# Layer-1 FFN of a vision tower: tokens normed and turned in the attention, results turned by VectorE and DRAM, pieces in a new order, and six attention buffers

## The chip, the cores and the metric

The kernel runs on one core of one Trainium2 chip. A core has TensorE (PE; PEld is its weight load), VectorE (DVE), ScalarE (ACT), GpSimd (POOL) and SyncE (SP), each with its own queue that is worked off in order; here SP issues nearly all transfers. The metric is the device time of one execution in microseconds (us); the time before is the median of three runs.

## The reference

32 images of 3x256x256 are cut into 256 patches of 16x16, and each becomes a token of 256 features. Two layers follow, each an attention and an FFN with a layer norm ahead of it and a residual around it. Layer 0 is a gated attention and a gelu FFN on 127 chosen tokens. Layer 1's attention works with phases (sine and cosine) and a causal sum. Layer 1's FFN is the last stage:

```python
sx = einsum('bsh,ndh->bnsd', x, hl_w) + hl_b          # 4 heads of 64
q = einsum('bnsd,neod->bneso', sx, wq)                # 4 experts
scores = einsum('bnesd,bntd->bnest', q, k) * d ** 0.5 + causal
out = softmax(scores) @ v                             # then gated over experts: mixed
resid = sx[arange(nh), arange(nh)]                    # image n, head n, for every image
hn = layernorm(mixed + resid, ln_g, ln_b)
hx = relu(fx @ fc1_w.T + fc1_b) @ fc2_w.T + fc2_b     # fx: hn by heads
fout = layernorm(hx + fx, fnorm_g, fnorm_b)
return fout * softmax(fout @ fgate_w.T) by heads
```

x is the normed token; the result is added to the unnormed one.

## The kernel before, in words

All 32 images stay in SBUF (`H`, tokens on the partitions, features along the row). The stages follow each other: patches to tokens (A), layer-0 attention (B), layer-0 FFN (C), layer-1 attention (D, to about 1245 us), layer-1 FFN (E, to the end). In all of them the order of instructions on each engine is the order in which the program is written. A matmul needs features on the partitions, so tokens must be turned first.

**Two ways of turning.** `feature_major` turns one image with four 128x128 transposes on TensorE into a bank of PSUM, and another engine copies them out. `blocks_turned` turns 32x32 blocks on VectorE and writes them to DRAM; `moved` reads them back with the blocks in their places, and gives a view of the tile in which runs of 32 columns lie 128 apart. B, C and D use the second way.

**Stage D** works on pairs of images, in steps t; `do(s, f)` runs f for pair u where t = 3u + s. So each f comes up once in three steps, and a pair passes: `norm_d`, `blocks_d` and `moved_d` (s = -1), `residual_d` on GpSimd (1), `hidden` (2, gelu), `phases` (3, tanh and sine: dturn, dz), `match` (4, dat), `memory` (5, reads the normed tokens dx), `output` (6), `add_output` and `stats_e` (7). dx has four buffers, two pairs. `norm_d` of a pair stands after `memory` of the pair two before it, whose buffers it takes. The first two pairs are normed in stage C; pair 0's tile dxT is loaded at step 1.

**Stage E** is cut into 93 pieces (`PIECES`), most of them on one engine. `ROUND` is one round, written out by hand: entries (-back, piece), so that image r + back has its piece in round r. Nine images are in flight. From `heads` of the last image on, the order is that of the list `END`. The pieces that matter here:

- `tokens` (VectorE, ex, L175) norms an image's tokens, `turn` (TensorE, L808) turns them, `turned` (ScalarE, exT, L1108) copies them out, and `heads` multiplies by hl. For the first four images `heads` also makes the residual `res`.
- `mixed` 0 and 1 (VectorE and GpSimd, L1289), `summed`, `squares`, `root`, `scaled` give er. `turn_e` turns er on TensorE, and `turned_e` (ScalarE, fxT, L1331) copies it out with the norm's factors.
- `features_moved` and `first_layer_out` move halves into the tile both by DMA; `second_layer` multiplies by W2; `head_gate` (small VectorE products, L1382 to L1406) and `last_norm` (VectorE L1411, L1414, L1425; GpSimd L1417, L1422) end the image. `later_keys` (GpSimd, L1208) masks the scores.

Weights of E are made in `prepare`, between the matmuls of stage C. After the images a check of value ranges decides whether a general path must be run (not in these executions).

Of the kernel before, what the change touches and what calls it, by code (L numbers as in the profile page):

```python
# [33 lines left out]
F32 = mybir.dt.float32  # L34
# [19 lines left out]
for _name, _k in [  # L54
    ("b_u", 4), ("b_base", 1), ("gamma", 2), ("beta", 2), ("b1", 8), ("bk1", 2), ("bq1", 2),
    ("bk2", 1), ("bq2", 1), ("ln_w", 2), ("ln_b", 2), ("hl_b", 2), ("fc1_b", 1), ("freq", 1),
    ("e_g", 1), ("e_b", 1), ("fn_g", 1), ("fn_b", 1), ("fc2_b", 1), ("attn_g", 1),
]:
    COLS[_name] = (_n, _k)
    _n += _k  # L60
# [20 lines left out]
def vit_tower(tc, a, out):  # L81
# [12 lines left out]
    H = [cpool.tile([P, NC, D], F32, name=f"h{b}") for b in range(B)]  # L94

# [517 lines left out]
    hl = load(pwe, "hl", nc.sync)  # L613
    cen, fg = load(pwe, "centre", nc.sync), load(pwe, "fg", nc.sync)
# [21 lines left out]
    W2 = pwe.tile([P, NH, YC], F32, name="W2")  # L636
    c2_row = pwe.tile([P, NH, YC], F32, name="c2_row")
# [15 lines left out]
    for i in range(2):  # L653
        s, t = slice(i * HD, (i + 1) * HD), slice((1 - i) * HD, (2 - i) * HD)
        nc.sync.dma_start(fc1[s, s], a["fc1"])
        nc.sync.dma_start(fc1_x[s, t], a["fc1"])
# [9 lines left out]
    def prepare():  # L666
# [29 lines left out]
        nc.gpsimd.memset(cg, 0.0)  # L696

# [47 lines left out]
        for i in range(2):  # L745
            s = slice(i * HD, (i + 1) * HD)
            nc.vector.tensor_copy(cg[s, :, i, :], p[s, 0 : 2 * NH].rearrange("p (k x) -> p k x", k=2))

# [10 lines left out]
        for i in range(2):  # L759
            t = slice((1 - i) * HD, (2 - i) * HD)  # L760
            for hp in range(2):
                nc.vector.tensor_copy(W2[t, 2 * hp + i, HD:], p[t, hp * NH : (hp + 1) * NH])
# [10 lines left out]
        for i in range(2):  # L773
            s, t = slice(i * HD, (i + 1) * HD), slice((1 - i) * HD, (2 - i) * HD)
            for hp in range(2):
                n = 2 * hp + i
                nc.vector.tensor_copy(W2[s, n, 0:HD], cen[s, s])
                nc.vector.tensor_copy(W2[s, n, HD:], cg[s, hp, i, :])
                nc.vector.tensor_copy(W2[t, n, 0:HD], f2[t, :])

# [29 lines left out]

    def normed_e(pool, b):
        x = pool.tile([P, NC, D], F32, name="ex")
        normed(x, b, st_e)
        return x

    def features(pool, x):
        xT = pool.tile([P, 2, N], F32, name="exT")
        nc.scalar.copy(xT.rearrange("p k n -> p (k n)"), feature_major(x))
        return xT

# [31 lines left out]
    with region_c:  # L852
# [57 lines left out]
        for t in range(END_C):  # L910
# [3 lines left out]
            if t == END_C - 2:  # L914
                for u in range(2):
                    norm_d(2 * u, pairs[u], px, "cx", 8)
                for u in range(2):
                    blocks_d(2 * u, pairs[u], p0, "cs", [P, 4, D], 2)
            step_c(t)
# [9 lines left out]
    st_e = new_stats("e")  # L929
    with (  # L930
# [97 lines left out]

        NP = B // 2
        for t in range(3 * (NP - 1) + 8):  # L1030
# [6 lines left out]
            if t == 1:  # L1037
                do(1, moved_d)
# [8 lines left out]
            if t != 4:  # L1047
                do(1, residual_d)
            do(2, hidden, 0)
# [13 lines left out]
            if t > 4:  # L1063
                do(-1, norm_d, p8, "dx", 4)
                do(-1, blocks_d, p8, "dxB", [P, 2 * NC, D], 1)
                do(-1, moved_d)
            if t == 3 * NP:
                output(B - 4, pairs[NP - 2], (0, 1, 2))
            else:
                do(6, output)  # L1070
            if t in (6, 9, 12):
# [6 lines left out]
    with (  # L1078
# [21 lines left out]
        def tokens(b, im):  # L1100
            im.x = normed_e(p1, b)

        def turn(b, im):
            im.pt = feature_major(im.x)

        def turned(b, im):
            im.xT = p1.tile([P, 2, N], F32, name="exT")
            nc.scalar.copy(im.xT.rearrange("p k n -> p (k n)"), im.pt)  # L1108

        def heads(b, im):  # L1110
            p = im.ph = bank()
            for hp in range(2):
                for k in range(2):
                    mm(p[:, hp * N : (hp + 1) * N], hl[:, k, hp * P : (hp + 1) * P], im.xT[:, k, :], k == 0, k == 1)
            if b < NH:
                p = bank()
                for c in range(NC):
                    for k in range(2):
                        mm(
                            p[:, c * HD : (c + 1) * HD], im.xT[:, k, c * P : (c + 1) * P],  # L1120
                            hl[:, k, b * HD : (b + 1) * HD], k == 0, k == 1,
                        )
                nc.vector.tensor_tensor(
                    res[:, :, b, :], p[:, 0 : NC * HD].rearrange("p (c d) -> p c d", c=NC),
                    over(row_e("hl_b")[:, b * HD : (b + 1) * HD], [P, NC, HD], 1), ALU.add,
                )
            if b == NH - 1:
                centred(res8, res8, NC * NH)
# [197 lines left out]
        def turn_e(b, im):  # L1326
            im.pt = feature_major(im.whole["er"].rearrange("p (c n) d -> p c (n d)", c=NC))

        def turned_e(b, im):
            im.fT = whole(im, "fxT", [P, 2, N])  # L1330
            nc.scalar.activation(  # L1331
                im.fT.rearrange("p k n -> p (k n)"), im.pt, AF.Identity, bias=col("e_b"), scale=col("e_g")
# [31 lines left out]
        def second_layer(b, im):  # L1364
            both, im.py = im.whole["both"], [bank() for _ in range(NC)]
            for c, p in enumerate(im.py):
                for n in range(NH):
                    for q in halves:
                        x = both[:, n % 2, n // 2, c * P + q.start : c * P + q.stop]
                        mm(p[q, n * YC : (n + 1) * YC], x, W2[:, n, :])  # L1370
# [37 lines left out]
        def last_norm(b, im, i):  # L1408
# [24 lines left out]
            (tokens,), (turn,), (turned,), (heads,), (heads_out,), (experts, 0), (experts_out, 0),  # L1433
# [18 lines left out]
            (-1, 77), (-1, 78), (-5, 21), (-4, 49), (-5, 27), (-1, 79), (-5, 30), (-6, 6), (-5, 13),  # L1452
            (-2, 92), (-6, 8), (-5, 20), (-5, 17), (-1, 80), (-3, 60), (-1, 81), (-1, 82), (-2, 69),
            (-5, 23), (-3, 61), (-2, 70), (-2, 68), (-7, 3), (-3, 62), (-1, 83), (-5, 24), (-4, 50),
            (-1, 84), (-5, 19), (-5, 26), (-1, 85), (-8, 1), (-1, 86), (-4, 51), (-5, 35), (-5, 33),
            (-5, 29), (-5, 36), (-5, 31), (-1, 87), (-5, 38), (-4, 52), (-1, 89), (-4, 53), (-1, 90),
            (-5, 43), (-3, 63), (-7, 4), (-9, 0), (-4, 54), (-1, 88), (-5, 41), (-5, 44), (-8, 2), (-3, 64),
            (-5, 46), (-4, 55), (-1, 91), (-2, 71), (-2, 73), (-5, 37), (-3, 65), (-4, 56), (-5, 25),
            (-5, 39), (-5, 34), (-5, 32), (-2, 72), (-5, 45), (-3, 66), (-4, 57), (-5, 42), (-5, 40),
            (-5, 47), (-6, 9), (-6, 12), (-4, 58), (-2, 74), (-3, 67), (-6, 16), (-6, 10), (-6, 18),  # L1460
            (-6, 22), (-6, 15), (-6, 11), (-2, 75), (-2, 76), (-5, 48), (-6, 28), (-7, 5), (-4, 59), (-7, 7),
            (-6, 14),
        )
        END = (
            (2, 19), (6, 83), (1, 17), (6, 84), (3, 50), (2, 24), (6, 85), (2, 26), (3, 51), (2, 29),
            (3, 52), (1, 14), (4, 62), (0, 4), (3, 53), (3, 54), (6, 86), (4, 63), (1, 23), (2, 33), (3, 55),
            (6, 87), (5, 71), (6, 89), (3, 56), (0, 30), (2, 25), (4, 64), (5, 72), (2, 37), (3, 57),
            (1, 29), (1, 20), (2, 38), (2, 41), (3, 58), (4, 65), (6, 88), (2, 32), (4, 66), (4, 67),
            (2, 34), (2, 31), (2, 35), (2, 45), (5, 73), (5, 74), (4, 92), (2, 40), (2, 36), (5, 75),
            (2, 42), (2, 46), (3, 59), (2, 39), (2, 44), (4, 69), (5, 76), (2, 43), (5, 77), (4, 70),  # L1470
            (2, 47), (6, 90), (1, 13), (5, 78), (1, 30), (1, 15), (0, 5), (1, 19), (5, 79), (1, 21), (3, 60),
            (1, 26), (5, 80), (0, 6), (1, 16), (2, 48), (5, 81), (5, 82), (6, 91), (1, 22), (2, 49), (1, 9),
            (2, 50), (2, 51), (5, 83), (1, 27), (5, 84), (1, 12), (0, 13), (0, 7), (2, 52), (3, 61), (5, 85),
            (1, 18), (1, 25), (2, 53), (1, 28), (1, 10), (2, 54), (1, 24), (5, 86), (2, 55), (1, 11),
            (4, 71), (3, 62), (2, 56), (3, 63), (5, 89), (1, 35), (1, 33), (4, 72), (0, 19), (1, 34),
            (2, 57), (3, 64), (3, 65), (0, 8), (1, 36), (2, 58), (4, 73), (4, 68), (1, 32), (4, 74), (1, 41),
            (1, 43), (4, 75), (1, 37), (3, 66), (5, 87), (1, 42), (1, 40), (1, 44), (1, 38), (1, 31),
            (0, 15), (2, 59), (5, 88), (3, 67), (1, 46), (3, 69), (4, 76), (1, 45), (0, 17), (2, 60),
            (1, 39), (1, 47), (2, 61), (0, 21), (0, 12), (3, 92), (0, 16), (4, 77), (3, 70), (2, 62),
            (1, 48), (1, 49), (0, 14), (0, 23), (2, 63), (0, 25), (4, 78), (1, 50), (0, 27), (4, 79), (0, 9),  # L1480
            (1, 51), (5, 90), (2, 64), (3, 68), (0, 18), (2, 65), (1, 52), (0, 22), (3, 71), (2, 66),
            (1, 53), (0, 29), (0, 10), (1, 54), (0, 11), (4, 80), (1, 55), (3, 73), (3, 72), (0, 24),
            (1, 56), (0, 20), (0, 28), (0, 36), (4, 81), (0, 31), (0, 35), (1, 57), (0, 26), (0, 38),
            (0, 37), (4, 82), (1, 58), (3, 74), (2, 67), (0, 34), (0, 33), (0, 44), (0, 46), (5, 91),
# [432 lines left out]
```

## Time and profile before

| | |
|---|---|
| median of 3 runs | 1897.08 us (1895.45 to 1898.73) |
| profiled execution | 1897.49 us, span 1895.8 us |
| TensorE busy | 1845.8 us (97%) |
| VectorE busy | 1350.6 us (71%) |
| ScalarE busy | 792.0 us (42%) |
| GpSimd busy | 758.1 us (40%) |
| mean granted TensorE clock | 0.985 |

A row of groups gives the line, engine and operation, the tiles written and read, partitions x elements, the count, then busy time and the mean of one in ns, then the engine's idle time before them and what ended it. A row of order of time gives start and length in us. Busy time counts overlapped instructions once. A matmul in 32-bit floats shows as two records; a transpose as one.

### The profile page before, as it was taken

How to read it: one execution, taken by the hardware profiler on the slowest of the kernel's cores; microseconds unless marked ns; L12 is line 12 of the kernel's file. 1: busy time of each engine (PE TensorE's matmuls, PEld its weight loads, DVE VectorE, ACT ScalarE, POOL GpSimd, SP SyncE). 2: the span in 40 equal slices, each digit the busy share in tenths (PEclk: the TensorE clock that was granted, in tenths of full speed). 3: DMA queues.
4: the chain of work that ended last, by engine and by line, in shares of the span. 5: the costliest groups of instructions: out<-in, count | busy, mean ns of one | idle time of the engine just before them, and what ended most of it. 6: DMA issues, size and time to landing. Idle time of an engine off the chain costs nothing.

```text
span 1895.8 us, 36643 instructions
## 1 busy us (share of the span) xinstructions
PE 1845.8 (97%) x14548; PEld 1305.8 (69%) x14548; DVE 1350.6 (71%) x3287; ACT 792.0 (42%) x1608; POOL 758.1 (40%) x792
## 2 busy tenths in 40 slices
PE   9999999999999999999899999999999999999993
PEld 8887566666666676766555555578787878788872
DVE  2335477878786574535387777645999999999988
ACT  0001222222222212122334444457888787878772
POOL 1224133434343344334253333324455554545453
PEclk9999999999999999999999999999999999999995
DMA  9440221212121143333221111101222222222212
GB/s 312 152 150 20 42 62 42 72 40 64 37 65 36 64 136 117 108 100 100 71 67 45 49 63 45 45 18 30 52 64 52 64 55 64 54 64 52 63 41 58
DMA packets 148354, 134.33 MB, mean 71 GB/s; under 512 B 68560, under 2 KB 123344, under 8 KB 147792
## 3 DMA queue, kind: packets, MB, share of 16 engines
q1 hardware_dynamic: 141456, 114.34, 21.4%
q0 software_dynamic: 6144, 16.79, 2.9%
q8 instruction: 117, 1.92, 0.4%
q10 hardware_dynamic: 576, 0.79, 0.1%
q14 instruction: 61, 0.50, 0.1%
HBM read 66.34 MB, written 40.89 MB: 57 GB/s over the span
## 4 chain that ended last, share of the span: by engine, by line
PE 92%; DVE 4%; DMA 2%; issue 1%; ACT 0%; SPq 0%; POOL 0%; DVEq 0%
PE bank L116 90%; PE bank L808 2%; DMA dxT<-c_turned 2%; PE bank L514 0%; DMA patch<-in_patches_dram 0%; DVE fout L1411 0%; DVE fout L1425 0%; DVE dx L835 0%; DVE eo L1289 0%; DVE six L124 0%; DMA b_turned<-blocks 0%; DMA bxT<-b_turned 0%; DVE ranges L1312 0%; DVE fout L1414 0%; DVE ey L1374 0%
## 5 line engine op out<-in xcount | busy, mean ns | idle before, releaser
L1208 POOL TENSOR_SCALAR_AFFINE_SELECT et<-et 128x512 f32<-128x512 f32 (+1 forms) x192 | 165.8, 876 | 203.1 <-ACT et L1199 201.1
L1199 ACT ACTIVATE et<-bank 128x512 f32<-128x512 f32 x384 | 207.7, 630 | 30.6 <-PE bank L116 30.3
L116 PE MATMUL bank<-ev,et 128*64 128x68 f32 (+1 forms) x6144 | 200.6, 226 | 0.0
L116 PEld LDWEIGHTS bank<-ev,et 128*64 128x64 f32 x6144 | 193.0, 138 | 5.7 <-issue 4.7
L116 PE MATMUL bank<-g,sx 64*128 64x512 f32 (+1 forms) x512 | 177.6, 486 | 0.0
L116 PE MATMUL bank<-g,sw 64*128 64x512 f32 (+1 forms) x512 | 177.2, 486 | 0.0
L116 PE MATMUL bank<-tokW,patch 128*128 128x256 f32 x768 | 167.9, 382 | 0.6 <-DMA patch<-in_patches_dram 0.6
L116 PEld LDWEIGHTS bank<-tokW,patch 128*128 128x128 f32 x768 | 147.2, 192 | 21.6 <-DMA tokW<-in_tokW_dram 1.4
L116 PE MATMUL bank<-bxT,w_wuv 128*128 128x512 f32 x300 | 132.9, 598 | 2.7 <-DMA bxT<-b_turned 2.7
L1228 ACT COPY eo<-bank 128x280 f32<-128x280 f32 x256 | 96.1, 395 | 70.0 <-PE bank L116 63.3
L862 ACT ACTIVATE hT<-bank,cols 128x512 f32<-128x512 f32 x64 | 44.0, 687 | 186.7 <-PE bank L116 186.7
L116 PEld LDWEIGHTS bank<-g,sx 64*128 64x128 f32 x512 | 93.2, 187 | 31.7 <-issue 22.9
L116 PE MATMUL bank<-wvo,dm 128*128 128x512 f32 x256 | 114.3, 599 | 0.0
L116 PE MATMUL bank<-w_wo,gT 128*128 128x256 f32 x512 | 113.2, 380 | 0.0
L116 PE MATMUL bank<-attn,bv 128*128 128x256 f32 x512 | 113.1, 379 | 0.0
L116 PE MATMUL bank<-w_w,hT 128*128 128x256 f32 x512 | 112.3, 380 | 0.0
L116 PE MATMUL bank<-xsel,w_w 128*128 128x512 f32 x256 | 111.4, 593 | 0.0
L116 PEld LDWEIGHTS bank<-attn,bv 128*128 128x128 f32 x512 | 97.4, 190 | 19.4 <-issue 7.2
L124 DVE BATCH_NORM_STATS2 six<-h 128x6 f32<-128x256 f32 x256 | 105.5, 412 | 4.4
L116 PEld LDWEIGHTS bank<-w_w,hT 128*128 128x128 f32 x512 | 97.1, 190 | 15.4 <-issue 2.9
L116 PEld LDWEIGHTS bank<-g,sw 64*128 64x128 f32 x512 | 93.3, 187 | 20.0 <-issue 9.9
L116 PEld LDWEIGHTS bank<-w_wo,gT 128*128 128x128 f32 x512 | 97.4, 190 | 13.2 <-DVE gT L487 0.2
(273 smaller groups left out, 3751.3 us busy)
## 6 DMA issues: line engine op xcount, KB each, us to landing
patch<-in_patches_dram SPq DMA_DIRECT2D x31, 768.0 KB, 4.7
dxT<-c_turned SPq DMA_DIRECT2D x16, 512.0 KB, 3.8
sw<-sx SPq DMA_DIRECT2D x64, 128.0 KB, 2.3
out_dram<-fout SPq DMA_DIRECT2D x32, 256.0 KB, 2.4
both<-fxT SPq DMA_DIRECT2D x62, 128.0 KB, 2.3
both<-hx SPq DMA_DIRECT2D x62, 128.0 KB, 2.3
b_turned<-blocks SPq DMA_DIRECT2D x56, 128.0 KB, 3.3
bxT<-b_turned SPq DMA_DIRECT2D x56, 128.0 KB, 3.1
```

What stands on the lines that cost most here:

```text
L116: nc.tensor.matmul(o, lhsT, rhs, start=first, stop=last)
L124: nc.vector.bn_stats(six, x)
L808: nc.tensor.transpose(p[:, o : o + P], x[:, c, k * P : (k + 1) * P], ident)
L862: nc.scalar.activation(s.hT[:, m, :], p, AF.Gelu_apprx_tanh, bias=col("b1", m))
L1199: nc.scalar.activation(t2[:, i, :], p, AF.Exp)
L1208: nc.gpsimd.affine_select(out=own, in_=own, pattern=[[0, 2 * n_e], [1, P]], compare_op=ALU.is_ge, fill=0.0, base=0, channel_multiplier=-1,)
L1228: nc.scalar.copy(im.o[:, g * OC : (g + 1) * OC], p[:, 0:OC])
```

## The change

The tokens of E are normed by ScalarE in stage D (`norm_e`, `norms_e`, L945 of the new file), turned by VectorE's blocks and written to DRAM (`blocks_e`). In E `features_in` loads them by one DMA an image, and `heads` reads the strided view, with hl's rows in the matching order. The last two pairs, whose attention ends too late, are done within E after `heads_out` of images 1 and 2. The residual of image b < 4 is taken from `sx` (which holds the bias) with an identity matmul, in a piece of its own.

er of all images but the last is turned by VectorE (`turn_e`), written to DRAM and read back (`moved_e`); `turned_e` puts the pieces in order. Within each pair of heads the features then stand in another order, so fc1, W2 and the factors get permuted copies; W2_last is for the last image, which is turned as before.

`ROUND` and `END` are new. In D dx has six buffers, `norm_d`, `blocks_d` and `moved_d` stand before `hidden` and `memory` of the same step, and pair 0's dxT is loaded in stage C.

```diff
@@ stage C
                 for u in range(2):
                     blocks_d(2 * u, pairs[u], p0, "cs", [P, 4, D], 2)
+                pairs[0].f = moved(
+                    px.tile([P, 4 * N], F32, name="blocks", bufs=1).rearrange("p (i x) -> p i x", i=4), pairs[0].d
+                )
             step_c(t)
@@ stage D
+    def norm_e(u, tiles):
+        xs = []
+        for b in range(2 * u, 2 * u + 2):
+            st, rs, i = at(st_e, b)
+            q = slice(i * NC, (i + 1) * NC)
+            low = spool.tile([P, NC], F32, name="e_low")
+            nc.vector.scalar_tensor_tensor(low, st[:, i, :, 0], -1.0, rs[:, q], ALU.mult, ALU.mult)
+            x = tiles[b % 2]
+            for c in range(NC):
+                nc.scalar.activation(
+                    x[:, c, :], H[b][:, c, :], AF.Identity, bias=low[:, c : c + 1],
+                    scale=rs[:, i * NC + c : i * NC + c + 1],
+                )
+            xs.append(x)
+        return xs
+        def norms_e(b0, s):
+            s.xs = norm_e(b0 // 2, [p8.tile([P, NC, D], F32, name="dex", bufs=2) for _ in range(2)])
+
+        def blocks_e(b0, s):
+            y = p8.tile([P, 2 * NC, D], F32, name="dxB", bufs=1)
+            blocks_turned(y.rearrange("p j d -> p (j d)"), s.xs, normed_d[b0 // 2])
-            if t == 1:
-                do(1, moved_d)
             if t != 4:
                 do(1, residual_d)
+            if t > 4:
+                do(-1, norm_d, p8, "dx", 6)
+                do(-1, blocks_d, p8, "dxB", [P, 2 * NC, D], 1)
+                do(-1, moved_d)
             do(2, hidden, 0)
             ...
-            if t > 4:
-                do(-1, norm_d, p8, "dx", 4)
-                do(-1, blocks_d, p8, "dxB", [P, 2 * NC, D], 1)
-                do(-1, moved_d)
             ...
+            if t < 3 * (NP - 2) + 9:
+                do(9, blocks_e)
+            if t < 3 * (NP - 2) + 8:
+                do(8, norms_e)
@@ stage E
-        def tokens(b, im):
-            im.x = normed_e(p1, b)
-        def turn(b, im):
-            im.pt = feature_major(im.x)
-        def turned(b, im):
-            im.xT = p1.tile([P, 2, N], F32, name="exT")
-            nc.scalar.copy(im.xT.rearrange("p k n -> p (k n)"), im.pt)
+        def features_in(b, im):
+            t = p2.tile([P, 4, P], F32, name="exT")
+            d = normed_d[b // 2].rearrange("i q (f j x) -> j (q f) i x", f=4, j=2)
+            nc.sync.dma_start(t, d[b % 2])
+            im.f = t.rearrange("p i (c k t) -> p k c i t", k=2, t=32)
+        def last_features(u):
+            ...
+        def residual(b, im):
+            if b >= NH:
+                return
+            s, p = halves[b % 2], bank()
+            for c in range(NC):
+                mm(p[:, c * HD : (c + 1) * HD], im.sx[s, b // 2, c * P : (c + 1) * P], ident[s, s])
+            nc.vector.tensor_copy(res[:, :, b, :], p[:, 0 : NC * HD].rearrange("p (c d) -> p c d", c=NC))
+            ...
         def turn_e(b, im):
-            im.pt = feature_major(im.whole["er"].rearrange("p (c n) d -> p c (n d)", c=NC))
+            if b == B - 1:
+                im.pt = feature_major(im.whole["er"].rearrange("p (c n) d -> p c (n d)", c=NC))
+                return
+            y = whole(im, "esq", G8, key="blocks").rearrange("p g d -> p (g d)")
+            nc.vector.transpose(
+                y.rearrange("p (f s t) -> p s f t", f=4, t=32),
+                im.whole["er"].rearrange("p (c k m) d -> p k c (m d)", c=2, k=2),
+            )
+            im.d = dram.tile([2, 4, 32, N], F32, name="er_turned", bufs=4)
+            nc.sync.dma_start(im.d.rearrange("m i q x -> (i q) m x"), y.rearrange("p (m x) -> p m x", m=2))
+        def moved_e(b, im):
+            if b < B - 1:
+                im.ft = p1.tile([P, 4, P], F32, name="fraw")
+                d = im.d.rearrange("m i q (h x) -> m (q h) i x", h=2)
+                for m, s in enumerate(halves):
+                    nc.sync.dma_start(im.ft[s], d[m])
         def turned_e(b, im):
             ...
             nc.scalar.activation(
-                im.fT.rearrange("p k n -> p (k n)"), im.pt, AF.Identity, bias=col("e_b"), scale=col("e_g")
+                im.fT.rearrange("p k (c i t) -> p (k c) i t", i=4, t=32),
+                im.ft.rearrange("p i (s t) -> p s i t", t=32),
+                AF.Identity, bias=col("e_b_t"), scale=col("e_g_t"),
             )
         PIECES = (
-            (tokens,), (turn,), (turned,), (heads,), (heads_out,), (experts, 0), (experts_out, 0),
+            (features_in,), (residual,), (moved_e,), (heads,), (heads_out,), (experts, 0), (experts_out, 0),
             ...
         ROUND = (
             ...
+            (-11, 42), (-8, 78), (-11, 43),
+            (-11, 37), (-12, 14), (-11, 46), (-11, 45), (-10, 65), (-11, 47), (-8, 79), (-12, 28), (-12, 15),
             ...
+        LATE = {1: B // 2 - 2, 2: B // 2 - 1}
         ...
                 do(b, images[b], *i)
+                if do == heads_out and b in LATE:
+                    last_features(LATE[b])
```

In the new round VectorE's order is, by piece and images back: gate_softmax 4 to 6 [10] among head_gate 8, 9 [7], last_norm 0 [7], mixed 0 [10], heads_zero and head_values_out [11], last_norm 1 [7], summed 0 [10], features_zero [8], summed 1, 2 [10], second_layer_out 0 [8], squares_sum 0 [10], second_layer_out 1 [8], last_norm 4 [7], squares_sum 1 and head_gate 0, 1 [8], scaled [10], gate_logits [11] among head_gate 2 to 4 [8], gate_softmax 0, 1 [11], turn_e [10], head_gate 6, 7 [8]. GpSimd's is mixed 1, last_norm 2, later_keys 1, last_norm 3, later_keys 5, 3, 0, 4, 2.

## The prediction

> **What bounds the kernel now.** I read the page's busy shares first, then the engines' busy time stage by stage, then the groups of ten steady rounds of the last stage, then waits and order of time.
>
> ```profile
> PE 1845.8 (97%) x14548; PEld 1305.8 (69%) x14548; DVE 1350.6 (71%) x3287; ACT 792.0 (42%) x1608; POOL 758.1 (40%) x792
> 905.00:1240.00 335.00, 324.66 (x1293) 176.73 (x1292) 228.97 (x566) 131.69 (x174) 127.27 (x136) 0.99 0.15 52
> 1500.00:1700.00 200.00, 200.00 (x3294) 161.39 (x3292) 193.48 (x433) 164.65 (x399) 104.86 (x98) 1.00 0.23 58
> 1800.00:1896.00 96.00, 62.27 (x952) 46.64 (x948) 80.92 (x201) 48.67 (x123) 42.86 (x36) 0.76 0.18 49
> ```
>
> The columns of the last three are PE, weight loads, DVE, ACT, POOL. TensorE sets the time almost everywhere. The layer-1 attention (905 to 1240) leaves it idle 10.3 us. In the layer-1 FFN it is never idle, at 18.72 us an image (the round's first matmuls at 1507.15 and, ten rounds on, at 1694.39). But VectorE is busy 97% there: a second bound just under the first. In the tail (from 1800) VectorE leads.
>
> The groups of those ten rounds (count, us, mean ns), and the order of time, show what the change touches:
>
> ```profile
> L808 PE MATMUL bank<-ident,er 128*128 128x128 f32 x40 | 6.6, 287 | 0.0
> L808 PE MATMUL bank<-ident,ex 128*128 128x128 f32 x40 | 6.0, 273 | 0.0
> L175 DVE TENSOR_SCALAR ex<-h,st_e,rs_e 128x256 f32<-128x256 f32 x20 | 13.2, 697 | 0.0
> L1289 DVE TENSOR_TENSOR eo<-eo,gate 128x1024 f32<-128x1024 f32 x10 | 28.2, 2817 | 0.0
> L1406 DVE TENSOR_TENSOR fv<-fv,fgate 128x8 f32<-128x8 f32 x10 | 9.5, 945 | 0.3
> ...
> 1525.27 0.60 PE L808 MATMUL bank<-ident,ex 128*128 128x128 f32 x4
> 1525.80 0.41 PE L116 MATMUL bank<-ev,et 128*64 128x72 f32 x6
> 1512.93 1.92 POOL L1289 TENSOR_TENSOR eo<-eo,gate 128x1024 f32<-128x1024 f32 x1 [3.03 <-DVE gate L1285]
> 1513.11 2.81 DVE L1289 TENSOR_TENSOR eo<-eo,gate 128x1024 f32<-128x1024 f32 x1
> 1450.42 1.52 DVE L1411 TENSOR_TENSOR fout<-ey,fv 128x512 f32<-128x512 f32 x1
> 1469.70 1.52 DVE L1411 TENSOR_TENSOR fout<-ey,fv 128x512 f32<-128x512 f32 x1
> 1487.87 1.52 DVE L1411 TENSOR_TENSOR fout<-ey,fv 128x512 f32<-128x512 f32 x1
> ```
>
> First, four transposes hold the stream from 1525.27 to 1525.80: 0.53 us (the er four, from 1514.02 to 1514.60: 0.58). Second, VectorE's times are stretched: 0.945 us for eight elements, 2.82 us for a product whose like takes 1.25 (L1297). Third, the three starts of L1411: after a round stretched to 19.28 us (the range check falls in it), the next takes 18.17, and the old grid is regained. So VectorE, when late, needs up to 18.17 us a round: only 0.55 under TensorE.
>
> **What the Trainium skill says.** "SBUF — State Buffer", section "Who interferes with whom": a VectorE instruction with two SBUF inputs, or in a 2-port mode, and a GpSimd one that reads SBUF lock each other out for a whole instruction. The trace agrees: VectorE's L1289 starts 0.18 us after GpSimd's half and ends 1.07 us after that ends. "VectorE: DVE Perf Modes", "The three transpose paths": VectorE turns 32x32 blocks only, so the blocks must be moved as well; here a 128x512 STREAM_TRANSPOSE takes 0.685 us (L197), with one input, so without the lock. "TensorE: Matmul & The Clock Gate", "Part 4: PE-mode transpose": some 275 ns; the row has 273, though pipelined each costs the stream 0.13 to 0.15. "DMA: Bandwidth & Descriptors", "Latency and other measured facts": about 2 us fixed; the like transfers here land in 2.3 to 3.8.
>
> **The change, part by part** (against the execution of 1897.49 us, span 1895.8; the median is 1897.08, 0.4 lower).
>
> *TensorE in the FFN.* The ex transposes go for all 32 images: 32 x 0.53 = 17.0 us. The er transposes go for 31; 28 of those lie before the tail: 28 x 0.58 = 16.2. The four residuals lose 8 passes each (0.84 us from 1267.18 to 1268.02 in order of time) for four of 64 columns (estimate 0.4): 1.8. In all 35 us; a steady round falls to 18.72 - 1.11 = 17.61. This is the floor.
>
> *VectorE in the FFN.* Busy 181.4 us in ten rounds, 18.14 a round. Its stretch: L1289 2.82 for 1.25, L1411 1.52 for 0.68, L1406 0.945 for 0.17 (its time in the disturbed round), L1404 and L1395 0.9 more than their free 0.15, ex 0.63 (two at 0.697; shortest 0.381), L1300 0.1: 4.8 us. Free of it: 13.3. The change takes ex's free 0.69 away and adds one transpose, 0.65: 13.25. The new order puts root (ScalarE) right between squares_sum and head_gate with nothing to fill; the two ScalarE steps take 0.53, so VectorE waits about 0.6 there, and 0.2 at squares_sum: 0.8 (now 0.58 idle in all). So a round needs max(17.61, 14.05 + c), c being the time lost to GpSimd. Now c without ex is 4.2; it is 0 if no pair collides, and nearly GpSimd's 9.7 busy us at the worst. The new order still lets GpSimd's half of L1289 go just ahead of VectorE's, with L1411 now between, and puts summed beside last_norm's GpSimd adds. I take c = 4.0, a little under today's: 18.05 us. That is 28 x (18.72 - 18.05) = 18.8 us, plus in the first four rounds, where VectorE is not full, the transposes and residuals: 4 x 0.53 + 1.8 = 3.9.
>
> *ScalarE in the FFN.* The exT copy (0.59) goes; fxT reads SBUF, about its 0.77. It has 164.7 of 200 busy: hidden.
>
> *DMAs and SP's queue.* Per round 7 issues become 11: exT, er_turned, two fraw. The write of er_turned is issued at a round's end and read a third of a round later (some 6 us): 2.6 us landing is covered. fraw lands (2.3 to 3.8) before turned_e near the round's end. Behind a late er_turned SP would hold out and fxT's move; uncovered it would be 1 to 2 us a round. DMA share 0.23 may near 0.4. I take 0.
>
> *Attention, six dx buffers.* TensorE waits for dxT 9.5 us: 5.0 at the start, then about 0.55 in every other pair and 1.2 once. The first dxT is now loaded before the last expert steps, and dx no longer waits for the matmuls that read the old buffers (2.85 us, below). I take all 9.5 as gained; 5 at least.
>
> *Attention, the tokens' norm.* Added per pair: two e_low and two transposes on VectorE, four 128x256 on ScalarE (0.44 each, from L963's 0.47), one DMA. The second pair of transposes falls where VectorE waits 1.42 us for d_rs: free. The norms do not:
>
> ```profile
> 1124.04 2.31 DVE L835 TENSOR_SCALAR dx<-h,rs_d,d_one 128x256 f32<-128x256 f32 x2 [2.85 <-PE bank L116]
> 1127.29 0.84 ACT L963 ACTIVATE dturn<-bank,cols 128x256 f32<-128x256 f32 x2 [1.36 <-PE bank L116]
> 1129.56 0.84 DVE L965 TENSOR_SCALAR dz<-dturn,cols 128x512 f32<-128x512 f32 x2
> 1132.42 1.06 ACT L970 ACTIVATE dz<-dz 128x1024 f32<-128x1024 f32 x1 [2.99 <-DVE dz L969]
> 1134.18 1.58 PE L116 MATMUL bank<-dz 64*128 64x256 f32 x16
> ```
>
> ScalarE's norms stand ahead of dturn and need e_low, which stands behind VectorE's dx and its transposes. Now dturn is done (1128.13) before VectorE comes to dz (1129.56); afterwards dz follows VectorE by e_low 0.3, norms 1.75, dturn 0.84 and handovers, 3.1 us. The slack is 0.7 (1133.48 to 1134.18). VectorE starts up to 2.85 us earlier, but GpSimd's residual adds (1122.3 to 1127.6) lock its dx out; I take 1.8. Left: 3.1 - 0.7 - 1.8 = 0.6 a pair, halved because a stalled TensorE gives the next pair's VectorE a head start: 0.3 x 13 = 4 us. Bounds 0 and 16. The attention nets -5.5.
>
> *Start and tail.* Eight norms (3.5 us) stand in ScalarE's queue among the first rounds, and the first tokens come by DMA: +1. In the tail three er transposes pass to VectorE (1.9 us), while the new order may mend some idle time: +1, bounds -5 and +5. The new weights of the preparation hide under the experts' matmuls.
>
> Sum: -18.8 - 3.9 - 5.5 + 2 = -26.2: 1897.5 - 26.2 = 1871.3, or 1871 beside the median.
>
> **The rivals.** *A, the floor:* the new order parts VectorE and GpSimd (c under 3.5) and dturn is not late: -35 - 9.5 + 2 = -42.5, 1855. For it: VectorE loses a contender; against it: the margin of 0.55. *B, the gain is locked away:* c near 4.5: the round is 18.55, the FFN gives 5 + 4, the attention 0 to 5: 1886. *C, slower:* the same lock, in the new order, costs more than now. Worked by hand, the waiting GpSimd instruction takes the port as soon as VectorE's ends (L1395 shows that, 0.59 for 0.15): L1289 loses 1.9, the first sum 1.05, last_norm and the other sums 1.5, the small products 1: c = 5.4, the round 19.45; 28 x 0.73 = 20 us more, less 9.4 elsewhere: 1908. It decides from a round of about 19.05 on (c = 5.0). *D:* TensorE's time doesn't fall because the matmul reading a strided exT is slower. Against it: the attention's matmuls already read dxT so: 0.594 us (w_wq), against 0.592 where the operand is contiguous (w_wuv, bxT).
>
> **How the numbers follow.** My case (1860 to 1881) 0.42, A 0.32, B (1881 to 1893) 0.17, C 0.08, D 0.01. A measurement of this kernel tells 0.2%, 3.8 us, from no change. Below 1893.3: 0.87; within: 0.05; above: 0.08. A reaches to 1850 with a better tail and B to 1890; these hold 0.8.
>
> **What would show it.** ex and L808 gone but for four; rounds of 17.6 (A) or 18.05 with TensorE a few per cent idle on ScalarE or VectorE; L1289, L1411 and the sums as the stretched VectorE rows; dxT gone from TensorE's waits, dz in it. Wrong if VectorE's stretch falls below 3.5 or above 5, or if fraw or exT appear in TensorE's chain.

## The result, and the profile after

The changed kernel takes 1882.48 us (median of four, 1881.05 to 1883.93) against 1896.45 for the kernel before on the same chip: ratio 0.9925, interval 0.9908 to 0.9942. That is 14 us less, where 26 were forecast; it lies in the range and in the band of rival B.

The busy shares and the same three stretches as before, for the changed kernel (columns PE, weight loads, DVE, ACT, POOL, then clock, DMA share, GB/s; the third stretch ends at 1880):

```profile
PE 1829.4 (97%) x14282; PEld 1286.5 (68%) x14282; DVE 1346.5 (72%) x3336; ACT 800.0 (43%) x1640; POOL 827.1 (44%) x792
905.00:1240.00 335.00, 330.26 (x1317) 179.75 (x1316) 251.59 (x639) 160.82 (x232) 129.46 (x138) 1.00 0.21 74
1500.00:1700.00 200.00, 199.77 (x3244) 159.10 (x3240) 181.98 (x426) 156.76 (x389) 130.72 (x97) 1.00 0.39 101
1800.00:1880.00 80.00, 46.91 (x776) 34.59 (x772) 69.14 (x176) 39.31 (x99) 35.81 (x28) 0.75 0.26 71
```

TensorE's idle time in the attention fell from 10.3 to 4.7 us. In the FFN it seems as full as ever, though two groups of four transposes a round are gone. Where the time went is read best from the first and last `heads` matmuls:

| | first heads | last heads | between | after the last | ten rounds / 10 |
|---|---|---|---|---|---|
| before | 1249.0 | 1805.9 | 556.9 | 89.9 | 18.72 |
| after | 1239.5 | 1792.1 | 552.6 | 87.2 | 18.62 |

(the last column but one is the span, 1895.8 and 1879.3, less the second). So all before the FFN gave 9.5 us, the rounds 4.3 and the tail 2.7. TensorE lost 1.11 us of transposes a round, and the round became 0.10 shorter.

The groups of ten rounds after (1511.86 to 1698.10) show VectorE, and the idle time ahead of its instructions:

```profile
L1318 DVE TENSOR_TENSOR eo<-eo,gate 128x1024 f32<-128x1024 f32 x11 | 32.3, 2941 | 0.0
L1326 DVE TENSOR_TENSOR two<-eo 128x1024 f32<-128x1024 f32 x10 | 22.9, 2292 | 0.0
L1341 DVE TENSOR_REDUCE ranges<-esq 128x8 f32<-128x512 f32 x20 | 13.7, 686 | 7.9 <-ACT esq L1337 7.9
L1337 ACT ACTIVATE esq<-er 128x512 f32<-128x512 f32 x10 | 6.3, 632 | 20.8 <-DVE er L1332 20.8
L1434 DVE TENSOR_TENSOR lg<-ey,fv 128x32 f32<-128x32 f32 x10 | 1.9, 192 | 5.5 <-ACT fv L1349 5.5
```

`mixed` (L1318) is stretched as before, `summed` 0 (L1326) now takes 2.29 us. VectorE waits for ScalarE's squares and factors, and ScalarE for VectorE's er: 2.1 us a round in which everything behind it in its queue stands still, `experts_out` and `outputs_out` among it. The waits of the same window, and the chain from 1225 to 1880 (two views, the second cut by the profile itself):

```profile
PEld bank L118 <- DVE ev L1203: 6.9, 10, 0.7
```

```profile
by line: DVE eo L1318 11.6%; DVE two L1326 8.8%; PE bank L118 6.5%; ACT eo L1257 6.5%; ACT esq L1337 4.9%; issue 4.2%; DVE er L1332 4.1%; ACT g L1190 3.9%; DVE er L1329 3.9%; DVE fout L1463 3.6%; DVE ev L1203 3.4%; DVE ranges L1341 3.3%; DV
```

The chain before ran through TensorE (90% of 1240 to 1896); now it goes from VectorE to ScalarE and back, and TensorE has 6.5% of it. Its own row says 100% busy all the same. Its wait is in the row of the weight loads: 0.69 us a round for `head_values_out` (ev).

### The profile page after: what moved, and what is told of

Read it like the earlier page. It is cut to its first block, busy times and chain, and to the rows that moved or that the text cites. A ratio compares the mean times of both kernels' runs of the same rounds, so it can differ in the third digit from the quotient of the medians.

```text
span 1879.3 us, 36625 instructions
## 1 busy us (share of the span) xinstructions
PE 1829.4 (97%) x14282; PEld 1286.5 (68%) x14282; DVE 1346.5 (72%) x3336; ACT 800.0 (43%) x1640; POOL 827.1 (44%) x792
## 5 line engine op out<-in xcount | busy, mean ns | idle before, releaser
L1237 POOL TENSOR_SCALAR_AFFINE_SELECT et<-et 128x1024 f32<-128x1024 f32 (+1 forms) x192 | 199.4, 1059 | 206.5 <-ACT et L1228 185.7
L118 PE MATMUL bank<-ev,et 128*64 128x72 f32 (+1 forms) x6144 | 204.2, 225 | 3.9 <-DVE ev L1203 2.3
L1228 ACT ACTIVATE et<-bank 128x512 f32<-128x512 f32 x384 | 199.6, 624 | 3.1 <-PE bank L118 1.7
L118 PE MATMUL bank<-g,sx 64*128 64x512 f32 (+1 forms) x512 | 194.4, 501 | 0.3 <-ACT g L1190 0.3
L118 PE MATMUL bank<-g,sw 64*128 64x512 f32 (+1 forms) x512 | 189.9, 501 | 0.9 <-DVE ev L1203 0.9
L118 PEld LDWEIGHTS bank<-attn,bv 128*128 128x128 f32 x512 | 97.2, 190 | 19.6 <-issue 7.2
L118 PEld LDWEIGHTS bank<-g,sx 64*128 64x128 f32 x512 | 88.1, 186 | 31.4 <-issue 21.8
L118 PEld LDWEIGHTS bank<-w_wo,gT 128*128 128x128 f32 x512 | 97.2, 190 | 13.4 <-DVE gT L489 0.2
L118 PE MATMUL bank<-w_wuv,bxT 128*128 128x512 f32 x240 | 105.4, 592 | 0.0
```

The costliest lines, as they stand in the source:

```text
L118: nc.tensor.matmul(o, lhsT, rhs, start=first, stop=last)
L1228: nc.scalar.activation(t2[:, i, :], p, AF.Exp)
L1237: nc.gpsimd.affine_select(out=own, in_=own, pattern=[[0, 2 * n_e], [1, P]], compare_op=ALU.is_ge, fill=0.0, base=0, channel_multiplier=-1,)
```

## The experiments

The question was where the other 12 us stayed: in VectorE's loop, in TensorE, or in the attention. Rounds are means of ten.

**1 and 2. Take VectorE's work away.** The two counts of zeros (a 0.67 us instruction each a round, for the range check) are left out, in the changed kernel and in the one before. Nothing else of the kernel depends on them but the check's flag.

```diff
-            count_zeros(im.sx, b)
+            pass
...
-            count_zeros(im.fT, B + b)
+            pass
```

> The changed kernel without the two counts of zeros per image in the layer-1 FFN (left out: the check for zero features; 1.35 us of VectorE's work a round, nothing on another engine). Theory V (VectorE's loop of work, lock and waits sets the round of 18.62 us): the round falls to between 17.6 and 17.8, near TensorE's floor of 17.61, the whole to about 1857 us. Theory T (TensorE is busy 186.03 of 186.24 us in ten rounds, so it is the bound and its matmuls have become slower): the round stays at 18.6, the whole at 1882.

> The kernel before without the same two counts (left out: the check for zero features). Both theories say that TensorE sets its rounds of 18.72 us: no change of the round; the whole falls by at most 3 us in the tail, where VectorE leads (1.35 us for each of two or three images), so 1894 to 1897.

Measured: changed kernel 1868.00 (ratio 0.9850, 0.9835 to 0.9865), round 18.05 in place of 18.62; kernel before 1896.66 (0.9991, 0.9983 to 1.0000), round 18.72 as it was. So VectorE bounded the changed kernel and not the one before. But 1.5 us of VectorE's work (0.75 with its read-out, twice) bought only 0.57, and not the 0.8 to 1.0 that was expected: something stops the round at 18.05.

**3. Fill VectorE's waits.** Three pieces of VectorE's (`last_norm` 4, `features_zero`, `scaled`) move to where it waits.

```diff
 VectorE, by piece and images back
-... summed0 [10], features_zero [8], summed1 ... squares_sum0 [10], second_layer_out1 [8], last_norm4 [7], squares_sum1, head_gate0, 1 [8], scaled [10]
+... summed0 [10], summed1 ... last_norm4 [7], squares_sum0 [10], second_layer_out1, features_zero, squares_sum1 [8], scaled [10], head_gate0, 1 [8]
```

> The changed kernel with three VectorE pieces of the round moved, so that VectorE has work while ScalarE makes the squares and the roots: last_norm 4 ahead of squares_sum 0, features_zero behind second_layer_out 1, scaled ahead of head_gate 0. Nothing is left out. Theory V: of the 1.41 us in which VectorE waits for squares and root each round most goes; the round falls to 17.6 to 17.8 and the whole to about 1857. Theory T: 1882, no change. A third reading (VectorE is held by GpSimd's lock alone, and the waits merely move): 1875 to 1882.

Measured: 1883.75 (0.9929, 0.9914 to 0.9945), round 18.64: nothing gained. In the waits of this kernel (1500 to 1700) that for the squares shrank from 7.9 to 2.2 us, and a new one stands instead:

```profile
DVE ranges L1280 <- ACT eo L1257: 7.3, 10, 0.7
```

A miss. The new wait is that of `gate_logits` for the last `outputs_out` in ScalarE's queue: the wait that was filled opened again elsewhere. Besides, L1329 without `features_zero` ahead of it grew from 0.97 to 1.46 us.

**4. Shorten ScalarE's leg of the loop.** `squares` 0 goes behind `experts_out` 1 and `outputs_out` 1, 2 in ScalarE's queue, so that these no longer wait for er.

```diff
 ScalarE
-outputs_out5, squares0 [10], experts_out1, outputs_out1, outputs_out2, squares1
+outputs_out5, experts_out1, outputs_out1, outputs_out2, squares0 [10], squares1
```

> The changed kernel with one ScalarE piece moved: squares 0 behind experts_out 1 and outputs_out 1 and 2 in the round, so that ScalarE does these while VectorE finishes er. Nothing is left out, VectorE's order is the same. Theory L (the round is set by a loop through two engines: er on VectorE, squares 0, then everything behind it in ScalarE's queue up to outputs_out 6, then gate_logits to er on VectorE): ScalarE's wait of 2.08 us for er is filled with 1.6 us of work, the loop shortens by 0.7 to 1.6 us, the round falls to 17.6 to 17.9, the whole to 1855 to 1864. Theory V (VectorE's own work and lock fill the round): at least 1878.

Measured: 1886.75 (0.9948, 0.9931 to 0.9965), round 18.65. A miss: the loop stayed as long. ScalarE no longer waits for er, but 1.2 us a round for VectorE's result of the second layer (`ey`), and TensorE's weight loads wait 1.0 us a round for ev in place of 0.7.

**5. Take the lock off `mixed`.** `mixed` 0 moves behind the count and the two instructions that take head_values out of PSUM. GpSimd's half of `mixed` is released by the same gate as before, so it now runs beside those.

```diff
 VectorE
-last_norm0 [7], mixed0 [10], heads_zero [11], head_values_out0, 1 [11], last_norm1 [7]
+last_norm0 [7], heads_zero [11], head_values_out0, 1 [11], mixed0 [10], last_norm1 [7]
```

> The changed kernel with mixed 0 on VectorE moved behind heads_zero and head_values_out 1, which don't contend with GpSimd, so that GpSimd's mixed 1 can run beside these. Nothing is left out. If the lock's cost is where the two meet: L1318 falls from 2.94 us to under 2, the round by about 1 us, the whole to 1855 to 1865. If GpSimd's next instruction takes the port in its place: the stretch moves to another row, the round stays over 18.3 and the whole over 1873.

Measured: 1869.74 (0.9861, 0.9845 to 0.9878), round 18.05. Order of time of the changed kernel, and then of this one:

```profile
1529.97 2.29 POOL L1318 TENSOR_TENSOR eo<-eo,gate 128x1024 f32<-128x1024 f32 x1 [0.43 <-DVE gate L1314]
1530.40 2.94 DVE L1318 TENSOR_TENSOR eo<-eo,gate 128x1024 f32<-128x1024 f32 x1
...
1534.41 0.29 PEld L118 LDWEIGHTS bank<-g,sw 64*128 64x128 f32 x2 [0.69 <-DVE ev L1203]
```

```profile
1526.94 2.29 POOL L1318 TENSOR_TENSOR eo<-eo,gate 128x1024 f32<-128x1024 f32 x1 [0.43 <-DVE gate L1314]
1527.98 0.88 DVE L1203 TENSOR_TENSOR ev<-bank,ones_row 128x320 f32<-128x320 f32 x2
1528.78 1.53 DVE L1318 TENSOR_TENSOR eo<-eo,gate 128x1024 f32<-128x1024 f32 x1
```

GpSimd's half takes its 2.29 us in both. In the first VectorE's half stands still beside it, and the count and `head_values_out`, for which TensorE waits, come after it. In the second these run beside GpSimd's half at their usual 0.68 and 0.88 us. Over ten rounds L1318 fell from 2.94 to 1.53 us and L1326 from 2.29 to 1.65; L1466 (`last_norm` 1) took 0.82 of that (0.70 to 1.53), L1332 0.46, L1329 0.20, which leaves the 0.57 by which the round fell. With no work removed, one moved piece gave some 12 us over the change. The round stops at 18.05 again.

**6. All of these together.** The edits of 4 and 5, with `last_norm` 4 and `scaled` earlier as in 3.

> Both of these moves, and last_norm 4 ahead of squares_sum 0 and scaled ahead of head_gate 0 (without moving features_zero). Nothing is left out. Theory L: the round reaches TensorE's floor, 17.6 to 17.7, the whole 1852 to 1858. Theory V: 1870 or more.

Measured: 1868.38 (0.9856, 0.9840 to 0.9872), round 18.03. The profile's chain from 1520 to 1580 is TensorE's alone. By it TensorE is the bound, at 18.03 and not at 17.61; but part of that is a hidden wait, as shown below experiment 7. This is the fastest full version: by the two ratios some 13 us under the changed kernel.

**7. Give er's turn back to TensorE.** er of all images is turned by TensorE, with two buffers for er; its features keep their old order.

```diff
-            if b == B - 1:
+            if True:
                 im.pt = feature_major(im.whole["er"]...)
                 return
...
-            if b < B - 1:
+            if False:
                 im.ft = p1.tile([P, 4, P], F32, name="fraw")
```

> The changed kernel with er of every image turned on TensorE, as before the change, ahead of outputs 6, with two buffers for er; no er_turned and no fraw. TensorE gets 0.58 us a round more (floor 18.19), VectorE 0.65 us less within the loop, and 3 of 11 DMAs go. Under theories L and V alike the round falls from 18.62 to between 18.2 and 18.3, the whole to 1869 to 1873: the turning of er on VectorE costs more than it brings. If the transposes' 0.58 us of TensorE still set the time: 18.62 or more, 1882 or more.

Measured: 1884.24 (0.9934, 0.9917 to 0.9950), round 18.60, where 18.2 to 18.3 was expected: a miss. TensorE is alone in the chain of 1520 to 1580 (97.2% matmuls, 2.9% the turn), and all full rounds are alike. The whole path of er through DRAM is worth nothing in the changed kernel (18.62 against 18.60), because VectorE's loop takes the place of what TensorE saved. That 18.60 less the turn's 0.58 is 18.02, as in experiment 6, is chance: here the outputs around the turn take 0.15 us more, there TensorE waits.

**Where TensorE's 0.41 us is.** The version of experiment 6 takes 18.02, and the prediction's floor was 17.61. But this kernel also has rounds of 17.86, with the same 298 matmul records in the same order: those that start at 1307.01 and at 1415.32. The changed kernel has two (17.86 and 17.88, from 1307), the version of experiment 5 four in a row, each among its first full rounds. So 18.02 is not TensorE's own time. Order of time of such a round, and of a later one:

```profile
1307.01 1.99 PE L118 MATMUL bank<-exT,w_hl_t 128*128 128x256 f32 x8
1322.65 1.10 ACT L1228 ACTIVATE et<-bank 128x512 f32<-128x512 f32 x2
1323.92 1.02 PE L118 MATMUL bank<-WV,sx 64*128 64x80 f32 x16
1324.87 0.70 PE L118 MATMUL bank<-exT,w_hl_t 128*128 128x256 f32 x2
```

```profile
1541.31 1.99 PE L118 MATMUL bank<-exT,w_hl_t 128*128 128x256 f32 x8
1557.13 1.10 ACT L1228 ACTIVATE et<-bank 128x512 f32<-128x512 f32 x2
1558.22 1.18 PE L118 MATMUL bank<-WV,sx 64*128 64x80 f32 x16
1559.33 1.99 PE L118 MATMUL bank<-exT,w_hl_t 128*128 128x256 f32 x8
```

head_values begins 16.91 us into both rounds. ScalarE's exponentials (`et`) let go of the second PSUM bank that it needs at 16.74 in the first and at 16.92 in the second. There head_values takes 1.11 us in place of 0.95, and every other piece is equal to 0.01. So 0.16 of the 0.41 is a wait for ScalarE, which itself waits 1.35 us a round for VectorE's `ey`. No row of waits sets it apart. In experiments 1 and 5 such a wait, for `g` of `experts_out`, stands in the outputs (4.67 us in place of 4.48).

The other 0.25 is in the rounds of 17.86 too. From start to next start: heads 1.83 us (before: 1.73), experts 1 0.96 (0.86, half of a pair's 1.73), the six scores together 5.37 (5.30); first_layer and head_values are 0.01 shorter each. All stand where pieces with 64 rows in their weights (scores, experts, head_values) meet pieces with 128. The old order had one block of pieces with 64 rows a round, the new one has two.

**8. One more meeting, in the kernel before.**

```diff
 TensorE
-outputs1, turn_e [3], head_values [6], scores0 [6]
+outputs1, head_values [6], turn_e [3], scores0 [6]
```

> The kernel before with one piece of TensorE's moved: head_values (16 products whose weights have 64 rows) ahead of turn_e (four turns with 128 rows) and not behind it, so that TensorE goes once more per round from 128 rows to 64 and back. All else stands. Theory S (a change of the rows costs TensorE 0.1 us or more each way, and the changed kernel's order has two such pairs a round where the kernel before has one): round 18.72 to between 18.92 and 19.1, the time up by 6 to 11 us, since this kernel waits for TensorE alone. Rival (the 0.41 us of the changed order comes from something else, as the two experts' pieces that are no longer neighbours): round 18.72, time within 2 us.

Measured: 1902.47 (1.0032, 1.0021 to 1.0042): 6.35 us slower by a swap of two neighbours. From its order of time:

```profile
1553.92 1.12 PE L116 MATMUL bank<-WV,sx 64*128 64x80 f32 x16
1554.98 0.66 PE L808 MATMUL bank<-ident,er 128*128 128x128 f32 x4
```

head_values goes from 0.95 to 1.05 us, the scores behind the turn take 0.06 more, and the round goes to 18.88, 0.16 more: just under what was expected for such a pair. So a second block explains some 0.16 of the 0.25, and by the rows alone 0.09 is left over.

**9 and 10. One block again.** An order of my own for the changed kernel: head_values, the scores and both experts in one block, then heads, first_layer and the outputs. In the first form `later_keys` 3 comes after outputs 4, which leaves that piece's causal mask out; the second has it back.

```diff
 TensorE
-head_values, heads, first_layer, scores5, 0, 4, experts1, outputs5, 2, second_layer, outputs1, 0, 3, 7, 4, 6, scores2, 3, experts0, scores1
+head_values, scores0, 4, 2, experts1, scores3, experts0, scores1, 5, heads, first_layer, outputs (9: 5, 2, 1, 0, 3, 4, second_layer, 7, 6; 10: 5, 0, 4, 2, 1, 3, second_layer, 7, 6)
```

> The changed kernel's pieces in an order of my own: TensorE's 64-row pieces in one block (head_values, scores 0, 4, 2, experts 1, scores 3, experts 0, scores 1, 5), then the 128-row ones (heads, first_layer, outputs 5, 2, 1, 0, 3, 4, second_layer, outputs 7, 6); VectorE's and ScalarE's pieces follow, the second layer's result is taken earlier, mixed0 stays behind heads_zero. Theory S (changes of the rows): TensorE's round of 18.02 falls to 17.6 to 17.75, and the time to 1856 to 1862, if ScalarE keeps up with a block that gives it 8.5 us of exponentials and experts' results in 7.8 us of TensorE; where it doesn't, TensorE waits for banks there and the round is 18.0 to 18.5, but the pieces' own slots (heads from 1.83 to 1.73, experts 1 from 0.96 to 0.86) still get shorter. Rival (not the rows): slots as they were, 18.02 or more.

> The order of a_order with its new waits mended: outputs in the order 5, 0, 4, 2, 1, 3, 7, 6 with second_layer ahead of 7, the masks of exponentials 1 ahead of GpSimd's half of mixed and those of exponentials 3 in the round before (in a_order they came after outputs 4, which so read unmasked exponentials), first_layer_out ahead of heads_out, root0 and scaled earlier. TensorE's 64-row pieces stand in one block again. Theory S (changes of the rows): TensorE alone would take 17.6 to 17.75 a round, by the slots of the pieces; time 1856 to 1864 if no new wait stands in the block, where ScalarE has 8.5 us of exponentials and results against 7.8 us of TensorE. If waits for ScalarE or GpSimd are left, 18.0 to 18.8 a round and 1868 to 1890, while the slots of experts 1 and head_values stay at 0.86 and 0.95 as in a_order. Rival (the rows cost nothing): slots of 0.96 and 1.11 come back.

Measured: 1916.42 (1.0107, 1.0085 to 1.0130) and 1890.20 (0.9963, 0.9952 to 0.9974). Both miss as times: the rounds are 19.9 and 18.8 us. From order of time of the first, and the waits (1500 to 1700) of the second:

```profile
1553.01 2.65 PE L118 MATMUL bank<-ev,et 128*64 128x72 f32 x80 [1.34 <-POOL et L1237]
1557.44 1.05 PE L118 MATMUL bank<-W,both 128*64 128x68 f32 x28 [1.35 <-DMA both<-hx]
```

```profile
DVE two L1326 <- POOL eo L1318: 25.4, 11, 2.4
ACT fxT L1381 <- DMA fraw<-er_turned: 16.9, 11, 1.9
```

In the first TensorE waits for the masks and for first_layer_out's transfer. In the second both are gone, but GpSimd does a mask ahead of its half of `mixed`, VectorE waits 2.3 us for it each round, and ScalarE 1.5 for er from DRAM. The slots answer the question of the rows: experts 1 is at 0.86 and head_values at 0.95 in both, as in the kernel before, while heads stays at 1.83 and was expected at 1.73. The shortest slots of the second add up to 17.70 us, 0.16 under the 17.86. A version that has this and no new wait was not found.

These runs agree in one working. The views print the shape of the weights, rows*columns: 64*128 (scores, experts, head_values), 128*64 (outputs, second_layer), 128*128 (heads, first_layer, transposes). Count the changes of shape in a round, take 0.16 us for each (experiment 8 less before) and 0.109 for a transpose (four in the stream start 0.33 us apart from first to last). Then the same time is left to the other pieces in all five (in the first two by construction):

| TensorE's own round | us | transposes | changes | left |
|---|---|---|---|---|
| before | 18.72 | 8 | 4 | 17.21 |
| experiment 8 | 18.88 | 8 | 5 | 17.21 |
| change, rounds of 17.86 | 17.86 | 0 | 4 | 17.22 |
| experiment 7 | 18.60 | 4 | 6 | 17.20 |
| experiment 10, shortest slots | 17.70 | 0 | 3 | 17.22 |

So the change removed eight transposes, 0.87 us, and left the number of changes of shape as it was. (The working was made after these runs. Its last three rows are its only test.) The prediction's 1.11 counted parts of these with the transposes: the last of each four takes 0.20 us up to the next piece and the first of er's 0.16, the others 0.11.

**11 and 12. The attention's edit alone, and the change without it.**

```diff
+                pairs[0].f = moved(...)          # stage C
...
-            if t == 1:
-                do(1, moved_d)
...
+            if t > 4:
+                do(-1, norm_d, p8, "dx", 6)     # with blocks_d, moved_d, ahead of hidden
...
-            if t > 4:
-                do(-1, norm_d, p8, "dx", 4)     # with blocks_d, moved_d, behind residual_d
```

> The kernel before with the attention's part of the change alone: six buffers for dx, norm_d, blocks_d and moved_d ahead of hidden and memory, pair 0's dxT loaded in the stage before. If the 9.5 us by which the attention ended earlier come from these: 1887 (9 to 10 us less than before), TensorE no longer waiting for dxT. If they need the new FFN as well: over 1893.

> The changed kernel with the attention's edit undone (four dx buffers, norm_d, blocks_d and moved_d behind residual_d, the first pair's tokens moved at t = 1), the FFN's rework kept with the norms and turns it does in the attention. Theory Q (the attention's edit brings practically the whole gain, the FFN's rework next to nothing): 1892 to 1896, the attention ends at or somewhat behind the kernel before's 1249.0, since VectorE's norms of the FFN come on top of the waits for dxT. Rival (the two parts share one gain, each would bring some 13 us alone): 1883 to 1886.

Measured: the kernel before with this edit alone 1884.49 (0.9938, 0.9924 to 0.9951), 13.1 us less: nearly the gain of the whole change. The changed kernel without it 1923.08 (1.0141, 1.0124 to 1.0158), 25 us more than before. Neither expectation of the latter held.

| | first heads | between | after the last |
|---|---|---|---|
| before | 1249.0 | 556.9 | 89.9 |
| attention's edit alone | 1237.5 | 556.9 | 88.4 |
| change without it | 1279.7 | 552.5 | 87.1 |
| change | 1239.5 | 552.6 | 87.2 |

The FFN's rounds and tail are worth 7.2 us without the edit and 5.5 with it. What differs is the attention: the FFN's norms there cost 30.7 us in the old order and 2.0 in the new. TensorE's waits in the change without the edit (905 to 1280), and in the change (905 to 1240):

```profile
PE bank L118 <- ACT dz L989: 27.9, 12, 2.7
PE bank L118 <- DMA dxT<-c_turned: 5.0, 1, 5.0
```

```profile
PE bank L118 <- DVE h L1041: 3.1, 2, 1.7
PE bank L118 <- ACT dz L992: 1.5, 2, 1.2
```

It is the late dz of the prediction, 2.3 us in each of twelve pairs, and the edit removes nearly all of it. (With the dxT waits of before, 9.5, now 5.0, these rows hold some 23 of the 30.7 us. A part of the rest lies in steps just behind the waits for dz, where w_wk's matmuls, 0.43 us apart as a rule, are four times 0.63 to 1.01 apart; the remainder is open.) Order of time of the change without the edit shows how it comes about:

```profile
1126.91 2.07 ACT L942 ACTIVATE dex<-h,e_low,rs_e 128x256 f32<-128x256 f32 x4 [2.98 <-DVE e_low L939]
1129.74 0.88 DVE L984 TENSOR_SCALAR dz<-dturn,cols 128x512 f32<-128x512 f32 x2 [2.85 <-ACT dturn L982]
1133.75 1.58 PE L118 MATMUL bank<-dz 64*128 64x256 f32 x16 [1.51 <-ACT dz L989]
```

e_low comes behind VectorE's dx and its transposes; the four norms hold ScalarE's queue; dturn, dz and TensorE follow. With six buffers and `norm_d` ahead of `hidden`, dx is made earlier in the step, and the same norms fit. (Which of the edit's parts does it, the buffers, the order or the first dxT, was not tested apart.) "The attention's edit brought 13 of the 14 us" is therefore true of one order of adding the parts only: added last, it brings 41.

## Why the prediction was half right

**The bound before** was read rightly: TensorE. 1.5 us less on VectorE changed nothing there, 0.16 us a round more on TensorE cost 6.

**The floor of 17.61** failed. It took the transposes out of TensorE's sum at 1.11 us, read from the first of four to the next piece. That stretch holds parts of the changes of the weights' shape at its ends, and the new order has as many of these as the old: eight transposes are 0.87, and the floor is 17.86. The first full rounds of the changed kernel ran at it; later ones wait. The ROUND was read for waits and the lock, not for TensorE's own order. Rival A's 17.6 was thus out of reach for this change.

**VectorE's round**, 13.25 + waits + c, had the right form and one wrong term. VectorE is busy 169.92 us in the ten rounds: 16.99, so c = 3.74 if the 13.25 holds (taken 4.0, bounds 3.5 and 5). The waits are 18.62 - 16.99 = 1.63 (taken 0.8). Hence 18.62 and not 18.05: the term was mis-sized by 0.83. It was sized as a sum of two hand-overs at two places. But VectorE and ScalarE wait for each other in a ring: filling its waits changed nothing (experiments 3 and 4), and taking VectorE's work or the lock out of it shortened the round (1 and 5).

**ScalarE "hidden"** failed for the same reason. Its 0.78 busy share of the FFN says that it has time, not that its queue has: `squares` 0 stands 2.1 us a round before results that TensorE and VectorE need, and ScalarE's instructions are in the chain. Which of them sets the length of the ring stays open, since filling the 2.1 us brought nothing (experiment 4).

**The lock's mechanism** was right. The Trainium skill's "SBUF — State Buffer", section "Who interferes with whom", names the pairs; L1318 at 2.94 and 1.53 us for the same work is the measure here. Of the rows forecast as stretched, `mixed` and the sums (L1318, L1326) were; L1411's successor L1463 was not (0.684). Rival C's hand working for L1318 (1.9 lost) and the first sum (1.05) came close to 1.69 and 1.04; of its smaller terms, 2.5 in all, about 1.0 came.

**DMAs and SP's queue** at 0: right. The share is 0.39 (some 0.4 forecast) and no transfer stands among TensorE's waits in the steady rounds. The strided exT (rival D) costs nothing either: 379 ns a record before and after.

**Attention:** forecast -5.5, measured -9.5. The dxT waits went to the last of 9.5 us; the edit alone gave 11.5. The norms' 4 became 2. The late dz was the right danger, and its cover the one named: the earlier dx.

**First rounds, start, tail:** -3.9, +1, +1 forecast. Of the 4.3 us between first and last heads the steady rounds hold 28 x 0.10 = 2.8, which leaves -1.5 for the first rounds with the start (-2.9 forecast). The tail gave 2.7 where a loss of 1 was forecast; why was not followed.

By the spans the change is -16.5 and the forecast -26.2. The 9.7 between are 28 x 0.57 = +16.0 in the steady rounds and +1.4 in the first ones, -4.0 in the attention and -3.7 in the tail. The medians, of other executions, stand 14.0 apart. Rival B's band held, though not its cause: c was no higher than forecast. That the total came within the range owes something to luck, since the attention and the tail gave 7.7 us more than forecast and covered nearly half of what the rounds fell short.

## What to carry to other kernels

When work leaves the bounding engine, price the whole new order of its queue, since what stands between two pieces may be a cost of their meeting that stays when one goes, and look for the ring of waits between the two next engines before you add up their busy times. Read the weight loads' waits where matmuls are modelled as full, and take an engine's own time from the shortest full round in the trace: a round that is longer with the same pieces in the same order has a wait in it, whatever the chain says. And test parts of a change in both orders of adding: a part that brings nothing alone may be what another part costs or saves.

## What the runs showed of the hardware beyond this

- A change of the weights' shape between matmul pieces (64*128, 128*64, 128*128) cost some 0.16 us: one more a round gave 18.88 for 18.72, one fewer 17.70 for 17.86. A 128x128 transpose in a stream cost 0.11.
- A row of TensorE with 186.03 of 186.24 us busy belonged to a kernel whose TensorE can do such rounds in 17.86, so ten in 178.6: its own first full rounds, with the same pieces in the same order.
- What the lock costs depends on which instructions meet: the same product took 2.94 us directly behind the gate that also released GpSimd's half, and 1.53 us behind a count and two additions out of PSUM (0.68 and 0.88 us, as ever).
